# Reordering the start and the first pair's layer-norm work, and writing three quarters of the last product by rows of tokens

## The chip, the cores and the metric

The kernel runs on one core of a Trainium2 chip. The core has a matrix engine (PE, with its weight loads shown apart as PEld), a vector engine (DVE), an activation engine (ACT), a general engine (POOL) and a sequencer that issues transfers (SP); ACT and POOL issue transfers too. Each engine works through its own instructions in program order and waits on semaphores for the others. The metric is device time in microseconds (us); the median over several runs counts.

## The reference

For eight batches of T = 512 tokens with H = 256 features the reference computes, all in fp32:

```
nx       = layer_norm(x) * gamma + beta
weights  = softmax((nx Wq)(ctx Wk)^T / 16)          # 64 context rows a batch
evidence = weights (ctx Wv)
combined = [nx, evidence, anchor]                   # anchor: one row a batch, the same for all tokens
probs    = softmax(combined router_W + router_b)    # 3 experts
h_e      = silu(combined e_w1[e] + e_b1[e])         # 512 wide
routed   = sum_e probs_e (h_e e_w2[e] + e_b2[e])
g        = sigmoid(silu(combined gate_w1 + gate_b1) gate_w2 + gate_b2)
out      = x + g * (routed out_w + out_b)
```

## The kernel before

The eight batches are worked in four pairs (`j` = 0 to 3, batches 2j and 2j+1). Features lie on partitions and tokens along the free axis, so a product of one 128-feature block with 512 tokens fills one PSUM bank. For each pair the kernel runs `gate_layer`, then `expert_layer` for experts 0, 1 and 2, then `outputs`. The products of a pair's two batches are shared by Winograd's form of a 2 by 2 block product: seven products in place of eight, with sums and differences of the inputs (`combine_x`) and of the weights (`combine_weights`, `combine_second` on POOL). In an expert layer `nx_product(n, 1..7)` names the seven products of group `n`; U, Y and Z are the PSUM banks in which they collect. `keep_part` (ACT) copies a part out of a bank, `add` (DVE, L827) adds a later one, `silu` (ACT, L821) finishes a chunk, and `weigh` (DVE, L872 and L868) multiplies finished chunks by the router's probabilities from a list of debts `late`.

All instructions are traced by hand in one order (`manual_schedule`), so each engine's queue is the order of the Python calls. In the loop over pairs `put(within, (e, point), step, ...)` hangs a step on a point of expert layer `e`: points W, A, B, C, D come in that order, and steps of one point run in the order of the puts. Work for the next pair is placed so in this pair's layers. For pair 0 that is:

- `statistics` (DVE) for batches 2 and 3, `deviation` (ACT, two square roots, with a change of the activation table),
- `normalize(b)` (DVE, L549 and L552: a reciprocal and four instructions of 256 columns), which overwrites x; `store_x(b)` (SP, four transfers) writes the result to DRAM and `regroup_x(b)` (SP, eight transfers) reads it back in blocks of 32 by 32 for `transpose_blocks` (DVE, L612) in `outputs`,
- `router_part(b)` (DVE, L590: four sums along x).

Before the loop stands the start: the loads, layer norm and transposes of pair 0 by PE, its scores and softmax. `turn_weights(0)` (DVE, L689 and L691, five block transposes) turns the softmax weights so that PE can use them in `evidence`; `anchor_rows(g)` multiplies the anchors by a first-layer weight on PE (L433) and transposes the result out of its PSUM bank on DVE (L438); `combine_x(0, ..., (i,))` makes one of the four differences (L624), number 2 in place over the second batch's first block. `misc()` hands out spare PSUM banks in turn, so a product that takes a bank must wait until the bank's last reader is done.

The last pair's end in `outputs` is written out apart. `finish_early` prepares r11 and r21 (residual and gate folded in), `experts(...)` is one second-layer product of six steps, `half_experts(y, n)` makes half of the first batch's first block, 256 tokens in the free axis with features on partitions. `finish_tokens(r11, ...)` turns it round on PE, by products with the identity that add r and the gated product in PSUM, copies and stores rows of tokens. `finish_late(r21, u, ...)` gates, adds, transposes in blocks of 32 and stores (four transfers on the ACT and SP queues). All these results use tiles of the tag `yb`, which has two buffers. Each fp32 product shows as two records on PE.

Of the kernel before, what the change touches and what calls it, by code (L numbers as in the profile page):

```python
# [8 lines left out]
F32 = mybir.dt.float32  # L9
AF = mybir.ActivationFunctionType  # L10
ALU = mybir.AluOpType
# [5 lines left out]
def kernel(  # L17
# [51 lines left out]
    nc = tc.nc  # L69
    P = 128  # L70
    B, T, H = x.shape
# [3 lines left out]
    NT = T // P  # L75
# [15 lines left out]
    work = ctx.enter_context(tc.tile_pool(name="work", bufs=2))  # L91
# [6 lines left out]
    def bank(i, name):  # L98
        return psum.tile([P, 512], F32, tag=f"b{i}", name=name)
# [4 lines left out]
    def misc(name):  # L104
        spare.append(spare.pop(0))
        return bank(spare[-1], name)
# [6 lines left out]
    ident = const.tile([P, P], F32, tag="ident", name="ident")  # L113
# [76 lines left out]
    r = 0  # L190
# [340 lines left out]
    S = {}  # L531
# [152 lines left out]
    def turn_weights(j):  # L684


        wT, w = work.tile([P, T], F32, tag="wT", name=f"wT_{j}", bufs=1), S["w", j]
        S["wT", j] = wT
        nc.vector.transpose(wT, w.rearrange("p g j c -> p (g j c)"))  # L689
        for i, h in SIDES:  # L690
            nc.vector.transpose(  # L691
                wT[side(i, 1 - h), h * NH : (h + 1) * NH],
                w[side(i, h), 1 - h, :, :].rearrange("p j c -> p (j c)"),
            )
# [91 lines left out]
    def product(ps, lhsT, rhs, start=False):  # L786

        nc.tensor.matmul(ps, lhsT, rhs, start=start, stop=True, skip_group_check=not start)  # L788
# [43 lines left out]
    def hidden(j, q, k, i):  # L832
        return S["h", i, 2 * q // RC][:, (2 * q + k) % RC, :]
# [165 lines left out]
    def outputs(j, steps):  # L999
# [7 lines left out]
        hg = [[S["hg", i, k] for i in range(2)] for k in range(2)]  # L1007
# [14 lines left out]
        u, z, y = (bank(i, f"ps_g{n}_{j}") for n, i in (("u", 0), ("z", 2), ("y", 4)))  # L1022
# [19 lines left out]
        NQ = NE // 2  # L1042
        pb = S["pb", j]

        def a(q, i, k):
            return w2o[:, 2 * q + k, i * P : (i + 1) * P]
# [60 lines left out]
        def gated(ps, i, row, ts):  # L1107
            g = S["hg", row, i][:, ts]
            nc.vector.tensor_tensor(g, ps, g, ALU.mult)
            return g  # L1110
# [4 lines left out]
            nc.vector.transpose(g, r)  # L1115
            store(g, i, row, slice(0, T), (nc.scalar, nc.sync))

        def finish_tokens(r, ps, i, row, n):

            ts = slice(n * T // 2, (n + 1) * T // 2)  # L1120
            pt = [misc(f"pt_out_{n}_{t}")[:, :P] for t in range(NT // 2)]
            for t in range(NT // 2):
                lo = n * T // 2 + t * P
                nc.tensor.matmul(pt[t], r[:, lo : lo + P], ident, start=True, stop=False)
            g = gated(ps, i, row, ts)
            y = work.tile([P, NT // 2, P], F32, tag="yb", name=f"y_{n}")
            for t in range(NT // 2):
                lo = n * T // 2 + t * P
                nc.tensor.matmul(pt[t], g[:, t * P : (t + 1) * P], ident, start=False, stop=True)
                (nc.scalar.copy if t else nc.vector.tensor_copy)(y[:, t, :], pt[t])  # L1130
                (nc.scalar if t else nc.sync).dma_start(
                    out[2 * j + row, lo : lo + P, i * P : (i + 1) * P], y[:, t, :]
                )

        r11, r22, r12, r21 = (
            bias_sum(f"r{i + 1}{row + 1}", i, row) for i, row in ((0, 0), (1, 1), (0, 1), (1, 0))
# [29 lines left out]
            run("P4")  # L1166
            return

        def half_experts(ps, n):
            ts = slice(n * T // 2, (n + 1) * T // 2)  # L1170
            for q in range(NQ):
                product(ps[:, : T // 2], a(q, 0, 1), hidden(j, q, 1, 0)[:, ts], start=q == 0)

        subtract((0, 1), ((1, 0), (0, 1)))
        experts(z, combo(S4), 1, 1)
# [2 lines left out]
        finish(r12, z, 0, 1)  # L1178
        experts(u, lambda q: a(q, 1, 0), 0, 0)
        finish(r22, u, 1, 1)  # L1180
        half_experts(y, 0)
        experts(u, lambda q: a(q, 1, 1), 0, 1)
        finish_tokens(r11, y[:, : T // 2], 0, 0, 0)
        y = bank(2, "ps_y3")
        half_experts(y, 1)
        finish_late(r21, u, 1, 0)
        finish_tokens(r11, y[:, : T // 2], 0, 0, 1)


    with tc.manual_schedule(engines=None):  # L1190
# [44 lines left out]
        spread_router_rows(0)  # L1235
        softmax(0)
        value_weights(0, 0, nc.vector.tensor_copy)
        turn_weights(0)
        combine_x(0, nc.vector, (2,))
        anchor_rows(E)  # L1240
        anchor_rows(0)
        combine_x(0, nc.vector, (3,))
        combine_weights(1)
        combine_weights(2)
# [8 lines left out]
        for j in range(NP):  # L1253


            within, between = {}, {}

            def put(where, n, step, *args):
                where.setdefault(n, []).append(lambda: step(*args))

            if j == 0:
                put(within, "gate", value_weights, 0, 1)
                put(within, (0, "A"), anchor_rows, 1)
                put(within, (0, "A"), router_logits, 0)
                put(within, (0, "A"), load_second, 1)
                put(within, (0, "B"), second_bias)
                put(within, (0, "C"), transpose_second, 0)
                put(within, (0, "C"), anchor_columns, 1)
                put(within, (0, "C"), anchor_rows, 2)
                put(within, (0, "C"), router_exp, 0)  # L1270
                put(within, (0, "D"), router, 0)
                put(within, (0, "C"), load_second, 2)
                put(within, (0, "D"), second_layer, 0)
                put(within, (0, "D"), spread_probabilities, 0)
                put(within, (0, "D"), combine_second, 0)
                put(within, (1, "A"), transpose_second, 1)
                put(within, (1, "B"), second_layer, 1)
                put(within, (1, "B"), combine_second, 1)
                put(within, (1, "C"), transpose_second, 2)
                put(within, (1, "C"), anchor_columns, 2)  # L1280
                put(within, (1, "D"), second_layer, 2)
                put(within, (1, "D"), combine_second, 2)
            if j:
                put(within, "gate end", spread_probabilities, j)
            if j and j + 1 < NP:
                put(within, (0, "B"), statistics, 2 * j + 3, 0, NT)
            put(within, (0, "C" if j == 0 else "B"), value_weights, j, 2)
            put(within, (1, "C"), load_x_blocks, 2 * j)
            put(within, (2, "A"), gate_differences, j)
            put(within, (2, "C"), load_x_blocks, 2 * j + 1)  # L1290
            if j + 1 < NP:
                b0, b1 = 2 * j + 2, 2 * j + 3
                if j == 0:
                    put(within, "gate", load_x, b0)
                    put(within, "gate", load_x, b1)
                if j + 2 < NP:
                    put(between, "begin", load_x, b0 + 2)
                    put(between, "begin", load_x, b1 + 2)
                put(within, (0, "A" if j else "D"), statistics, b0, 0, NT)
                if j == 0:  # L1300
                    put(within, (1, "A"), statistics, b1, 0, NT)
                for i in range(2):
                    put(within, (0, "D") if j else (1, "C"), deviation, j + 1, i)
                for b, n in ((b0, (1, "W") if j else (1, "D")), (b1, (1, "W") if j else (2, "W"))):
                    put(within, n, normalize, b)
                    put(within, n, store_x, b)
                put(within, (1, "A") if j else (2, "A"), router_part, b0)
                put(within, (1, "C") if j else (2, "A"), regroup_x, b0)
                put(within, (1, "D") if j else (2, "C"), router_part, b1)
                put(between, "begin", transpose_blocks, b0)  # L1310
                put(between, "gate", regroup_x, b1)
                put(between, "begin", value_weights, j + 1, E)
                put(between, "begin", store_router_rows, j + 1)
                put(between, "begin", spread_router_rows, j + 1)
                put(between, "P5", transpose_blocks, b1)
                put(between, "P2", scores, j + 1)
                put(between, "P2", combine_x, j + 1, nc.gpsimd)
                put(between, "P7", softmax, j + 1)
                put(between, "P7", value_weights, j + 1, 0)
                put(between, "P7", router_logits, j + 1)  # L1320
                put(between, "P3", value_weights, j + 1, 1)
                put(between, "P3", turn_weights, j + 1)
                put(between, "P3", router_exp, j + 1)
                put(between, "P4", router, j + 1)
            gate_layer(j, within)
            for e in range(E):
                expert_layer(j, e, within)
            outputs(j, between)


# [32 lines left out]
```

## Time and profile before

| what | us |
|---|---|
| median of 3 runs | 472.14 (472.06 to 472.33) |
| the profiled execution, its own time | 472.42 |
| the span of that execution in the profile | 470.6 |
| PE busy in the span | 461.1 (98%) |
| DVE busy | 362.1 (77%) |
| ACT busy | 213.3 (45%) |
| POOL busy | 95.0 (20%) |
| last transfer issued, landed (from the span's start) | 467.29, 469.08 |

The profile is of one execution; 1.8 us of its time lie around the span. PE's clock was granted in full almost throughout (0.999). A busy time counts an instruction from start to end; PE's records overlap, so the spacing of their starts is the better measure of PE's pace. A line such as "92.00 0.68 DVE L827" in a timeline gives the start and the duration in us, the engine and the source line, then the operation, the tile written, the tiles read, the shapes, how many instructions are merged, and in brackets the idle time ahead of it with what ended it.

### The profile page before, as it was taken

What the parts mean: (1) busy time and instruction counts of PE and PEld (TensorE: products, weight loads), DVE (VectorE), ACT (ScalarE), POOL (GpSimd) and SP (SyncE); (2) the same over time, 40 slices, a digit from 0 to 9 for tenths busy, and PEclk for the clock granted to TensorE, in tenths of its full rate; (3) what the DMA queues carried; (4) which work ended last, traced back from release to release, by engine and by line L of the source; (5) the groups of instructions that cost most, each with busy time, mean ns of one, the idle gap of its engine ahead of it and who ended that gap; (6) DMA issues with size and microseconds to landing.
All of it is one profiled execution on the core that took longest, in us unless ns stands there. A gap on an engine that the chain in (4) does not pass through costs nothing.

```text
span 470.6 us, 4723 instructions
## 1 busy us (share of the span) xinstructions
PE 461.1 (98%) x1455; PEld 209.8 (45%) x1455; DVE 362.1 (77%) x669; ACT 213.3 (45%) x368; POOL 95.0 (20%) x133
## 2 busy tenths in 40 slices
PE   9989999989999999999999999999999999999996
PEld 7534546334444344444444344444444344444454
DVE  3875646999899659978889669888989724787972
ACT  3335655548221476458220476458130455457000
POOL 6536123201072300001062300001062300000020
PEclk9999999999999999999999999999999999999999
DMA  9998830375111424732011333712011480000013
GB/s 277 288 166 152 123 136 0 80 139 94 7 22 22 80 101 103 124 87 45 6 24 22 58 121 79 123 23 45 7 22 22 69 201 0 0 0 1 0 22 67
DMA packets 119351, 34.86 MB, mean 74 GB/s; under 512 B 106060, under 2 KB 116352, under 8 KB 118816
## 3 DMA queue, kind: packets, MB, share of 16 engines
q1 hardware_dynamic: 115312, 27.02, 29.5%
q0 software_dynamic: 2128, 6.78, 5.0%
q10 hardware_dynamic: 1888, 0.79, 0.6%
q8 instruction: 11, 0.18, 0.2%
q14 instruction: 12, 0.10, 0.1%
HBM read 27.17 MB, written 7.39 MB: 73 GB/s over the span
## 4 chain that ended last, share of the span: by engine, by line
PE 67%; DVE 26%; issue 3%; DMA 3%; POOL 0%; ACT 0%; DVEq 0%; POOLq 0%; ACTq 0%
PE ps_u L788 32%; PE ps_z L788 12%; PE ps_y L788 12%; DVE h L1063 5%; PE ps_gu L788 3%; DVE h L872 3%; PE ps_vw L763 3%; DVE r L1094 2%; DVE yb L1095 2%; DVE r L1093 2%; DVE wT L691 1%; PE ps_w2o L494 1%; PE ps_gz L788 1%; DMA scr_small<-in_L_xcond_router_W_dram 1%; DMA scr_small<-in_L_xcond_e_b_dram 1%
## 5 line engine op out<-in xcount | busy, mean ns | idle before, releaser
L872 DVE TENSOR_TENSOR h<-h,pb 128x512 f32<-128x512 f32 x96 | 61.9, 693 | 6.0 <-ACT h L821 6.0
L788 PE MATMUL ps_u<-h,w2o 128*128 128x512 f32 x144 | 64.1, 594 | 0.0
L788 PE MATMUL ps_u<-nxT,w 128*128 128x512 f32 x112 | 55.9, 608 | 0.5 <-ACT h L830 0.5
L821 ACT ACTIVATE h<-h,abias 128x512 f32<-128x512 f32 x72 | 49.2, 718 | 15.1 <-DVE h L827 14.7
L788 PE MATMUL ps_z<-wT,vw 64*128 64x512 f32 x104 | 49.5, 605 | 0.0
L1096 POOL TENSOR_TENSOR yb<-yb,xb 128x512 f32<-128x512 f32 x14 | 18.4, 1314 | 146.1 <-DVE yb L1095 120.6
L788 PE MATMUL ps_z<-h,w2s 128*128 128x512 f32 x96 | 42.6, 593 | 0.2 <-DVE r L1079 0.2
L830 ACT COPY h<-ps_u 128x512 f32<-128x512 f32 x48 | 27.9, 581 | 30.7 <-PE ps_u L788 30.4
L788 PEld LDWEIGHTS ps_u<-h,w2o 128*128 128x128 f32 x144 | 27.1, 190 | 32.6 <-issue 29.2
L827 DVE TENSOR_TENSOR h<-h,ps_y 128x512 f32<-128x512 f32 x24 | 16.4, 681 | 25.0 <-PE ps_y L788 25.0
L1063 DVE TENSOR_TENSOR h<-h,h 128x1024 f32<-128x1024 f32 x24 | 34.3, 1483 | 0.0
L408 POOL DMA_DIRECT2D vrd<-vw x8 | 5.0, 628 | 143.6 <-ACT vw L770 143.6
L788 PEld LDWEIGHTS ps_u<-nxT,w 128*128 128x128 f32 x112 | 19.8, 189 | 30.6 <-issue 24.4
L821 ACT ACTIVATE h<-ps_u,abias 128x512 f32<-128x512 f32 x24 | 16.5, 687 | 28.5 <-PE ps_z L788 28.2
L827 DVE TENSOR_TENSOR h<-h,ps_z 128x512 f32<-128x512 f32 x24 | 16.1, 683 | 16.8 <-PE ps_z L788 16.7
L788 PE MATMUL ps_u<-wT,vw 64*128 64x512 f32 x56 | 28.2, 617 | 0.5 <-DVE hg L827 0.4
L788 PEld LDWEIGHTS ps_z<-h,w2s 128*128 128x128 f32 x96 | 18.2, 190 | 23.5 <-issue 21.8
L788 PE MATMUL ps_z<-T,ws 128*128 128x512 f32 x56 | 28.6, 592 | 0.0
L788 PE MATMUL ps_y<-nxT,w 128*128 128x512 f32 x56 | 28.6, 592 | 0.0
L763 PE MATMUL ps_vw<-w,vT 128*128 128x512 f32 (+1 forms) x64 | 27.0, 544 | 1.5 <-DVE ar L438 1.5
L788 PE MATMUL ps_u<-T,w 128*128 128x512 f32 x56 | 26.7, 594 | 1.5 <-DVE h L827 1.5
L788 PE MATMUL ps_y<-wT,vw 64*128 64x512 f32 x56 | 27.0, 597 | 0.0
(233 smaller groups left out, 796.4 us busy)
## 6 DMA issues: line engine op xcount, KB each, us to landing
pb<-pd POOLq DMA_DIRECT2D x4, 1536.0 KB, 6.6
xb<-in_x_dram SPq DMA_DIRECT2D x64, 64.0 KB, 2.4
out_dram<-yb SPq DMA_DIRECT2D x56, 64.0 KB, 2.0
w<-in_L_xcond_e_w_dram SPq DMA_DIRECT2D x6, 512.0 KB, 9.3
x<-in_x_dram SPq DMA_DIRECT2D x24, 128.0 KB, 3.2
xd<-x SPq DMA_DIRECT2D x24, 128.0 KB, 2.3
xg<-xd SPq DMA_DIRECT2D x48, 64.0 KB, 2.3
scr_wa<-in_L_xcond_e_w_dram SPq DMA_DIRECT2D x3, 512.0 KB, 15.2
```

The source lines that it names most:

```text
L408: nc.gpsimd.dma_start(S["vrd", j][i].rearrange("e c -> c e"), S["vw", j][row_half(i), R0:])
L763: nc.tensor.matmul(ps, vT[:, k, j * 2 * CT : (j + 1) * 2 * CT], w1[:, KH + k, n0:n1], start=(k == 0), stop=(k == KH - 1),)
L788: nc.tensor.matmul(ps, lhsT, rhs, start=start, stop=True, skip_group_check=not start)
L821: nc.scalar.activation(h, h if src is None else src, AF.Silu, bias=abias[:, c, 2 * j + i : 2 * j + i + 1])
L827: nc.vector.tensor_tensor(h, h, part, ALU.add)
L830: nc.scalar.copy(chunk(n, i, d), part)
L872: nc.vector.tensor_tensor(h, h, S["pb", j][:, i, :, 2 * q // RC, :], ALU.mult)
L1063: nc.vector.tensor_tensor(d, p, m, ALU.subtract)
L1093: nc.vector.tensor_tensor(r, r, ps, ALU.add)
L1094: nc.vector.tensor_tensor(r, r, S["hg", row, i], ALU.mult)
L1095: nc.vector.transpose(yb, r)
L1096: nc.gpsimd.tensor_tensor(yb, yb, S["xb", 2 * j + row][:, i, :], ALU.add)
```

## The change

Three places change.

1. In the start, `anchor_rows(E)`, `anchor_rows(0)` and `combine_x(0, ..., (2,))` are called ahead of `turn_weights(0)`, not behind it.
2. For pair 0, `deviation` moves from point C to point B of expert layer 1. `normalize` and `store_x` of both batches are at point C of layer 1 (before: batch 2 at D of layer 1, batch 3 at W of layer 2). `regroup_x(2)` is at D of layer 1 (before: A of layer 2). `router_part(2)` is at C of layer 2 (before: A of layer 2), ahead of `router_part(3)`, which stays there. For the later pairs all points stay as they are.
3. In the last pair's end only the first 128 tokens of the split block keep the old way (`finish_tokens`, one tile). For the other 384 the gate and r11 are turned round ahead of time (`turn_rest`: six PE transposes into two banks, two ACT copies), and the product itself is made with tokens on partitions (`token_experts`: the hidden chunk is the weight operand and the 128 columns of `w2o` the moving one). `finish_rows` multiplies and adds on DVE, in two instructions of 128 by 128, and stores.

```diff
-        def finish_tokens(r, ps, i, row, n):
-
-            ts = slice(n * T // 2, (n + 1) * T // 2)
-            pt = [misc(f"pt_out_{n}_{t}")[:, :P] for t in range(NT // 2)]
-            for t in range(NT // 2):
-                lo = n * T // 2 + t * P
-                nc.tensor.matmul(pt[t], r[:, lo : lo + P], ident, start=True, stop=False)
-            g = gated(ps, i, row, ts)
-            y = work.tile([P, NT // 2, P], F32, tag="yb", name=f"y_{n}")
-            for t in range(NT // 2):
-                lo = n * T // 2 + t * P
-                nc.tensor.matmul(pt[t], g[:, t * P : (t + 1) * P], ident, start=False, stop=True)
-                (nc.scalar.copy if t else nc.vector.tensor_copy)(y[:, t, :], pt[t])
-                (nc.scalar if t else nc.sync).dma_start(
-                    out[2 * j + row, lo : lo + P, i * P : (i + 1) * P], y[:, t, :]
-                )
+        def finish_tokens(r, ps, i, row):
+
+            pt = misc("pt_out")[:, :P]
+            nc.tensor.matmul(pt, r[:, :P], ident, start=True, stop=False)
+            g = gated(ps, i, row, slice(0, P))
+            nc.tensor.matmul(pt, g, ident, start=False, stop=True)
+            y = work.tile([P, P], F32, tag="yb", name="y_tokens")
+            nc.scalar.copy(y, pt)
+            nc.scalar.dma_start(out[2 * j + row, :P, i * P : (i + 1) * P], y)
...
-        def half_experts(ps, n):
-            ts = slice(n * T // 2, (n + 1) * T // 2)
+        def turn_rest(r):
+
+            rest = work.tile([P, 2, NT - 1, P], F32, tag="xg", name="rest", bufs=1)
+            for n, part in enumerate((S["hg", 0, 0], r)):
+                pt = misc(f"pt_rest_{n}")[:, : T - P]
+                for t in range(1, NT):
+                    nc.tensor.transpose(pt[:, (t - 1) * P : t * P], part[:, t * P : (t + 1) * P], ident)
+                nc.scalar.copy(rest[:, n, :, :].rearrange("p t c -> p (t c)"), pt)
+            return rest
+
+        def token_experts(ps, t):
+
             for q in range(NQ):
-                product(ps[:, : T // 2], a(q, 0, 1), hidden(j, q, 1, 0)[:, ts], start=q == 0)
+                product(ps, hidden(j, q, 1, 0)[:, t * P : (t + 1) * P], a(q, 0, 1), start=q == 0)
+
+        def finish_rows(rest, ps, t, queue):
+            y = work.tile([P, P], F32, tag="yb", name=f"y_rows_{t}")
+            nc.vector.tensor_tensor(y, ps, rest[:, 0, t - 1, :], ALU.mult)
+            nc.vector.tensor_tensor(y, y, rest[:, 1, t - 1, :], ALU.add)
+            queue.dma_start(out[2 * j, t * P : (t + 1) * P, :P], y)
...
-        half_experts(y, 0)
+        for q in range(NQ):
+            product(y[:, :P], a(q, 0, 1), hidden(j, q, 1, 0)[:, :P], start=q == 0)
+        rest = turn_rest(r11)
         experts(u, lambda q: a(q, 1, 1), 0, 1)
-        finish_tokens(r11, y[:, : T // 2], 0, 0, 0)
-        y = bank(2, "ps_y3")
-        half_experts(y, 1)
+        finish_tokens(r11, y[:, :P], 0, 0)
+        tokens = [bank(b, f"ps_tokens_{b}")[:, :P] for b in (2, 0, 5)]
+        for t in range(1, NT):
+            token_experts(tokens[t - 1], t)
         finish_late(r21, u, 1, 0)
-        finish_tokens(r11, y[:, : T // 2], 0, 0, 1)
+        for t in range(1, NT):
+            finish_rows(rest, tokens[t - 1], t, nc.scalar if t % 2 else nc.sync)
...
-        turn_weights(0)
-        combine_x(0, nc.vector, (2,))
         anchor_rows(E)
         anchor_rows(0)
+        combine_x(0, nc.vector, (2,))
+        turn_weights(0)
         combine_x(0, nc.vector, (3,))
...
                 for i in range(2):
-                    put(within, (0, "D") if j else (1, "C"), deviation, j + 1, i)
-                for b, n in ((b0, (1, "W") if j else (1, "D")), (b1, (1, "W") if j else (2, "W"))):
-                    put(within, n, normalize, b)
-                    put(within, n, store_x, b)
-                put(within, (1, "A") if j else (2, "A"), router_part, b0)
-                put(within, (1, "C") if j else (2, "A"), regroup_x, b0)
+                    put(within, (0, "D") if j else (1, "B"), deviation, j + 1, i)
+                for b in (b0, b1):
+                    put(within, (1, "W") if j else (1, "C"), normalize, b)
+                    put(within, (1, "W") if j else (1, "C"), store_x, b)
+                put(within, (1, "C") if j else (1, "D"), regroup_x, b0)
+                put(within, (1, "A") if j else (2, "C"), router_part, b0)
                 put(within, (1, "D") if j else (2, "C"), router_part, b1)
```

## The prediction

> **What bounds the kernel now.** I read the page first, then PE's own waits, then the timelines of the three places that the diff touches. On the page two lines matter:
>
> ```profile
> PE 461.1 (98%) x1455; PEld 209.8 (45%) x1455; DVE 362.1 (77%) x669; ACT 213.3 (45%) x368; POOL 95.0 (20%) x133
> DMA  9998830375111424732011333712011480000013
> ```
>
> PE is the bound, so a change pays only where PE stands still or where the end comes after PE. Slices 6 and 7 of the DMA row (70 to 94 us) are nearly empty: transfers put there meet no traffic. PE's waits from 10 to 130 us:
>
> ```profile
> PE ps_u L788 <- DVE h L827: 1.5, 1, 1.5
> PE ps_vw L763 <- DVE ar L438: 1.5, 1, 1.5
> PE ps_u L788 <- ACT h L830: 0.5, 1, 0.5
> ```
>
> These three are at 98.34, 32.13 and 93.97 us. From 130 us to the end's 462 us, PE's starts leave no gap above 0.4 us. The first stop, PE and DVE:
>
> ```profile
> 29.59 1.02 PE L788 MATMUL ps_z<-nxT,ws 128*128 128x512 f32 x2
> 32.13 1.98 PE L763 MATMUL ps_vw<-w,vT 128*128 128x512 f32 x4 [1.52 <-DVE ar L438]
> 28.48 0.71 DVE L689 STREAM_TRANSPOSE wT<-w 128x512 f32<-128x512 f32 x1
> 29.23 1.78 DVE L691 STREAM_TRANSPOSE wT<-w 32x256 f32<-32x256 f32 x4
> 31.03 0.69 DVE L624 TENSOR_TENSOR nxT<-nxT 128x512 f32<-128x512 f32 x1
> 31.64 0.44 DVE L438 STREAM_TRANSPOSE ar<-ps_ar 128x64 f32<-128x64 f32 x2
> ```
>
> The value product needs a bank that L438 empties only after L689, L691 and L624. The second stop, and what DVE does up to the next meeting with PE:
>
> ```profile
> 92.60 0.69 DVE L996 TENSOR_TENSOR hg<-hg,hg 128x512 f32<-128x512 f32 x1
> ...
> 97.00 0.68 DVE L827 TENSOR_TENSOR h<-h,ps_y 128x512 f32<-128x512 f32 x1
> 97.60 1.28 DVE L827 TENSOR_TENSOR h<-h,ps_u 128x512 f32<-128x512 f32 x2
> ...
> 106.84 0.69 DVE L1016 TENSOR_TENSOR hg<-g_r,ps_gz 128x512 f32<-128x512 f32 x1 [0.68 <-PE ps_gz L788]
> 107.71 0.69 DVE L1016 TENSOR_TENSOR hg<-g_r,ps_gu 128x512 f32<-128x512 f32 x1 [0.18 <-PE ps_gu L788]
> ...
> 118.41 3.49 DVE L1063 TENSOR_TENSOR h<-h 128x1024 f32<-128x1024 f32 x3
> ```
>
> DVE is full from 74.0 to 127.7 us but for 0.86 us. PE's S2 product starts at 119.69, just behind the first L1063: there DVE, not PE, sets the pace. The end:
>
> ```profile
> 462.93 2.76 PE L788 MATMUL ps_y<-h,w2o 128*128 128x256 f32 x12
> 466.20 0.71 PE L1129 MATMUL pt_out<-ident,hg 128*128 128x128 f32 x4
> 467.29 0.36 ACTq L1131 DMA_DIRECT2D out_dram<-y  x1
> ```
>
> The last store is issued at 467.29 and lands 1.8 us later, at 469.08; what follows is fixed.
>
> **What the Trainium skill says.** "SBUF — State Buffer", Who interferes with whom: a DVE instruction with two SBUF inputs and a GpSimd one that reads SBUF exclude each other. The trace agrees: three L872 at 80.56 take 2.95 us beside POOL's `combine_second` (80.87 to 85.2), against 0.69 for one alone. "DMA: Bandwidth & Descriptors", Anatomy of one DMA: most of a fixed 2 us is the write's receipt, so a buffer is free only at landing. The small stores here land after 1.6 to 1.8 us. "TensorE: Matmul & The Clock Gate", Back-to-back issue gap: loads and products overlap, spacing depends on both. Here four records with 128 columns (462.04 to 462.48) come at 0.11 us each, load included. "ScalarE: Activation LUTs", What ACT_TABLE_LOAD costs: 1283 ns; the trace has 1.28.
>
> **Part 1, the start: -1.78 us.** PE's order stays. On DVE the two L438 come at 28.48 (0.44), the difference 2 to 29.6, `turn_weights` (0.71 + 1.78) to 32.1, difference 3 to 32.7. The value product starts in step at 30.45 (0.43 a record after 29.59 and 30.02), not at 32.13; a stop also costs 0.10 on restart (32.13 to the next load 32.67, not 0.43). Sum 1.78. Next in line: `evidence` needs the turned weights, due at 33.12 instead of 34.90, ready at 32.1; 1.0 us of cover. The value copy on ACT and all DVE adds follow PE. What is not moved, the loads, has slack: the router rows land by about 41 and are read at 43.98 (then 42.2), second-layer weights by 43 and read at 50.38. PE has no idle from there to 90 and DVE's full stretch starts when PE releases it at 74.0, so the gain lasts. Bounds: 1.4 (a load binds) to 1.8.
>
> **Part 2, pair 0's layer norm: -1.03 us.** Square roots: on ACT nothing lies between the old and new place, both follow the `w2o` copy at 73.14; table load, two roots, done 75.54; cost 0. `normalize` of both batches (0.2 + 4 x 0.35 = 1.55 each) now follows L486 and L443, 76.85 to 79.95, ahead of ten weighings. Behind them wait the weighings, then two `add` of Z (86.30 to about 87.75) and ACT's two `silu` behind those (to 89.8, needed by nobody before 91.4). `add` of Y at 92.00 has the same work ahead of it as before, so the 0.78 us stop at 93.97 stays. POOL still meets two-input instructions at 80.87: same 1.7 us of contention, taken as 0 (+-0.3). SP's eight stores leave at 78.5 and 80.0, not at 86.41 and 91.52, the eight reads follow by 87; the queue's next work is later anyway. POOL's memset (0.11) is covered by its idle time.
>
> The four sums of batch 2 (`router_part`, L590, 0.47 each with the read of the accumulator, 95.26 to 97.00) leave this place: Y's second add runs at 95.26, U's two at 95.86 and 96.46. PE's product 4, due at 96.65, waits for the first: released at 96.6 instead of 98.3. PE gains up to 1.79. But both batches' sums now come in one piece up to 100.54, and everything on DVE behind them is where it was, until the gate: L1016 no longer waits, 105.47, 106.07, 106.67, transposes at 107.28 for 108.31. That is 1.03 us, and L1063 and PE's S2 product move by just that (119.69 to 118.66); PE, 1.79 ahead, stands 0.76 there. After it DVE idles 2.6 us at 130.29, so 1.03 stays. Bounds: 0.5 (contention) to 1.79 (DVE finds slack).
>
> **Part 3, the end: +0.45 us.** PE before its last full product: 12 records at 0.11 (1.32) for 2.59, plus six transposes (eight took 0.87 at 19.25) 0.66: -0.61, so that product ends at 461.43, not 462.04. Two ACT copies of 384 columns (512 take 0.58) lie in ACT's idle time. Then four records 0.44 and 36 at 0.11: tokens ready on PE at 463.19, 464.51, 465.83. DVE: `finish_late` 461.63 to 463.78, its stores on ACT to 464.76; rows 1 at 463.75 to 464.36, store at 464.79.
>
> The price is in the buffers. `yb` has two. The tiles r12, r22, tokens, rows 1, rows 2, rows 3 take them in turn, so the multiplication of rows 3 overwrites rows 1 and must await its landing. No wait of this kind shows before; bounds: 464.79 + 1.7 = 466.5 if it overtakes, 467.4 if it queues fully behind the `finish_late` stores, whose landings take 2.4 to 2.6 us. I take 467.1, as it is behind two of them on its queue. Then multiply and add (0.29 each, nearest row the 128x128 copy, + 0.03) and issue: 467.8, landed 469.55. Against 469.08 that is +0.45; bounds -0.1 to +0.8. Without the wait: product seen at 466.03, issued 466.67, landed 468.4, -0.7.
>
> **Sum:** 472.42 - 1.78 - 1.03 + 0.45 = 470.06 for the profiled execution. The median of the runs is 0.28 lower: 469.8.
>
> **Rivals.** *A, more:* rows 3 doesn't wait (the buffers go otherwise), or pair 0 keeps all of 1.79. The first alone gives 472.14 - 1.78 - 1.03 - 0.7 = 468.6, the second alone 472.14 - 1.78 - 1.79 + 0.45 = 469.0, both 467.9. For: PE's gap is 1.79. Against: two buffers, and 119.69. *B, less:* contention or the late Z adds eat part 2, or the landing is late: -1.78 - 0.3 + 0.8, 470.9. *C, slower:* weight loads set the pace of the 48 records with 128 columns. The groups give 190 ns for one load, and 256 columns run at 0.215. At 0.215 the end is 48 x 0.105 = 5.0 later than the unwaited 468.4: 473.4, +4.3; with -2.81 the median is 473.6. It decides from about 0.18 us a record. Against: the identity products and transposes at 0.11. *D, no change:* a load that I take for early paces the start, so that part 1 returns nothing: -1.03 + 0.45 = -0.58, with B's losses -0.3 + 0.8 = +0.5, so 471.6 to 472.6. For: the DMA row is at 9 up to 24 us. Against: from 33 to 90 us no wait of PE or DVE ends on a transfer.
>
> **Numbers.** Forecast 0.56, A 0.18, B 0.16, C 0.04, D 0.06. 0.2% (0.94 us) is about what a measurement of this kernel can tell from no change. Faster by more: forecast, A, B: 0.90; within: D, 0.06; slower: C, 0.04. The predicted time is the forecast's, 469.8. The range takes in A's single cases and B with a little beyond: 468.3 to 471.0; it leaves out A's double case, C and D.
>
> **What would show it.** Right: no wait of L763 on L438, evidence near 33.1; no wait of PE on L827 near 96.6 but a longer one on L1063, near 117 in the new clock; a DVE wait on a store from `yb` ahead of the last multiplication of 128 by 128, about 1.1 us. Wrong: 128-column products at 0.2 us; the same gap at 98 with DVE full ahead of it; a last store that lands before 468.4 less 2.8.

## The result and the profile after

| | us |
|---|---|
| after, median of 14 runs | 471.11 (470.96 to 471.42) |
| before, median of 14 runs beside them | 472.37 (472.02 to 474.72) |
| ratio after to before | 0.9965, 95% interval 0.9953 to 0.9977 |
| the profiled execution of after: its time, its span | 471.00, 468.87 |

The kernel is faster, by less than forecast. The ratio is one of means, and three of the runs of before lay at 474.4 to 474.7: it says 1.65 us, the medians say 1.26. By the ratio, the 472.14 from which the prediction started becomes 470.5 (469.9 to 471.1), by the medians 470.9. Both lie inside its range of 468.3 to 471.0, near its upper end, and above its 469.8; the median of after itself, 471.11, lies 0.1 above the range.

Page of after, busy time and DMA row, then PE's waits from 10 to 130 us (total, times, longest):

```profile
PE 459.8 (98%) x1473; PEld 209.8 (45%) x1473; DVE 363.7 (78%) x672; ACT 214.0 (46%) x369; POOL 97.6 (21%) x133
...
DMA  8989933532012405812011414702011570000013
```

```profile
PE ps_u L788 <- ACT h L830: 0.8, 1, 0.8
PE ps_u L788 <- DVE h L1063: 0.8, 1, 0.8
```

PE is still the bound. Of its three stops two are gone, those on L438 and L827. The one on L830 has grown from 0.5 to 0.8, and L1063 is new at 116.97, the place that the prediction gave it. The timeline of after, at the start (PE, DVE):

```profile
29.29 1.02 PE L788 MATMUL ps_z<-nxT,ws 128*128 128x512 f32 x2
30.14 1.88 PE L763 MATMUL ps_vw<-w,vT 128*128 128x512 f32 x4
...
32.81 0.69 PE L788 MATMUL ps_y<-wT,vw 64*128 64x512 f32 x1
...
28.19 0.45 DVE L438 STREAM_TRANSPOSE ar<-ps_ar 128x64 f32<-128x64 f32 x2
...
30.02 1.80 DVE L691 STREAM_TRANSPOSE wT<-w 32x256 f32<-32x256 f32 x4
```

The value product follows at PE's pace (0.85 us after the line above it), since L438 comes first; the turned weights are ready at 31.8, ahead of `evidence` at 32.81. The layer-norm stretch (DVE, POOL):

```profile
80.86 1.10 DVE L868 TENSOR_TENSOR h<-h,h 128x512 f32<-128x512 f32 x1
81.89 3.48 DVE L872 TENSOR_TENSOR h<-h,pb 128x512 f32<-128x512 f32 x3
...
90.21 0.68 DVE L827 TENSOR_TENSOR h<-h,ps_y 128x512 f32<-128x512 f32 x1
...
104.40 0.68 DVE L1016 TENSOR_TENSOR hg<-g_r,ps_gz 128x512 f32<-128x512 f32 x1
...
105.60 1.29 DVE L612 STREAM_TRANSPOSE nxT<-xg 128x512 f32<-128x512 f32 x2
...
78.78 2.63 POOL L233 TENSOR_TENSOR w2s<-w2o 128x256 f32<-128x256 f32 x1 [4.17 <-ACT w2o L499]
```

DVE's two-input instructions stretch beside POOL's `combine_second`, and POOL's first instruction takes 2.63 us for 0.95 before. At the gate L1016 no longer waits. The end (PE, ACT's queue, DVE):

```profile
459.18 4.18 PE L788 MATMUL ps_tokens<-w2o,h 128*128 128x128 f32 x36
...
462.22 3.93 ACTq L1181 DMA_DIRECT2D out_dram<-y_rows  x2
...
461.57 0.29 DVE L1179 TENSOR_TENSOR y_rows<-ps_tokens,rest 128x128 f32<-128x128 f32 x1 [0.47 <-DMA out_dram<-y_tokens]
...
465.14 0.29 DVE L1179 TENSOR_TENSOR y_rows<-ps_tokens,rest 128x128 f32<-128x128 f32 x1 [2.35 <-DMA out_dram<-y_rows]
```

DVE stands idle for 2.35 us, up to 465.14, until rows 1 have landed; PE was done at 463.4, so 1.8 us of this lie behind PE's end. The last store is issued at 465.79 and lands at 467.36.

To compare executions I divide them at fixed places: the first `ps_vw` record behind L438 ("start"), the beginning of the last z product ("z": 443.89 before, 441.19 after; PE runs in step with small constant gaps from 130 us up to there), the landing of the last store, the end of the span, the time. From the last landing to the end of the span is the "tail".

| stretch | forecast | measured |
|---|---|---|
| up to `evidence` (34.90 to 32.81) | -1.78 | -2.09 |
| from there to z | -1.03 | -0.61 |
| from z to the last landing (25.19 to 26.17) | +0.45 | +0.98 |
| from there to the end of the span (1.57 to 1.51) | 0 | -0.06 |
| outside the span (1.77 to 2.13) | 0 | +0.36 |
| sum (472.42 to 471.00) | -2.36 | -1.42 |

### The profile page after: what moved, and what is told of

Read it like the earlier page. It is cut to its first block, busy times and chain, and to the rows that moved or that the text cites. A ratio compares the mean times of both kernels' runs of the same rounds, so it can differ in the third digit from the quotient of the medians.

```text
span 468.9 us, 4767 instructions
## 1 busy us (share of the span) xinstructions
PE 459.8 (98%) x1473; PEld 209.8 (45%) x1473; DVE 363.7 (78%) x672; ACT 214.0 (46%) x369; POOL 97.6 (21%) x133
## 4 chain that ended last, share of the span: by engine, by line
PE 70%; DVE 25%; issue 3%; DMA 1%; ACT 0%; DVEq 0%
PE ps_u L788 31%; PE ps_z L788 12%; PE ps_y L788 11%; DVE h L1063 5%; DVE h L872 4%; PE ps_vw L763 3%; PE ps_gu L788 3%; DVE r L1094 2%; DVE yb L1095 2%; DVE r L1093 2%; PE ps_w2o L494 1%; PE ps_gz L788 1%; DVE wT L691 1%; DVE h L868 1%; DVE r L1073 1%
## 5 line engine op out<-in xcount | busy, mean ns | idle before, releaser
L830 ACT COPY h<-ps_u 128x512 f32<-128x512 f32 x48 | 27.9, 581 | 30.5 <-PE ps_u L788 30.1
L827 DVE TENSOR_TENSOR h<-h,ps_y 128x512 f32<-128x512 f32 x24 | 16.4, 683 | 25.0 <-PE ps_y L788 21.1
L1063 DVE TENSOR_TENSOR h<-h,h 128x1024 f32<-128x1024 f32 x24 | 34.3, 1483 | 0.0
L827 DVE TENSOR_TENSOR h<-h,ps_z 128x512 f32<-128x512 f32 x24 | 16.1, 684 | 16.8 <-PE ps_z L788 16.7
L788 PE MATMUL ps_u<-T,ws 128*128 128x512 f32 x56 | 26.7, 594 | 0.0
```

Of the source, the lines that this page charges most:

```text
L827: nc.vector.tensor_tensor(h, h, part, ALU.add)
L830: nc.scalar.copy(chunk(n, i, d), part)
L1063: nc.vector.tensor_tensor(d, p, m, ALU.subtract)
```

## The experiments

**Each part by itself.** Each kernel is the one before with a single part of the change: `start_only` part 1, `norm_only` part 2, `end_only` part 3.

```diff
# start_only
-        turn_weights(0)
-        combine_x(0, nc.vector, (2,))
         anchor_rows(E)
         anchor_rows(0)
+        combine_x(0, nc.vector, (2,))
+        turn_weights(0)
# norm_only: only the edits of deviation, normalize, store_x, regroup_x, router_part
# end_only: only finish_tokens, turn_rest, token_experts, finish_rows and their calls
```

> The kernel before with part 1 alone. Theory (each part does its own sum): 1.8 us faster than before, the value product no longer waits for L438, every later meeting of PE and DVE moves by the same 1.8. Rival (a load or the DVE stretch of pair 0 takes it back): under 1.0 us faster, with a new wait of PE between 33 and 120 us.

> The kernel before with part 2 alone. Theory: 0.6 us faster than before, PE's stop at 98.34 gone, the stop at 93.97 some 0.3 longer, a new stop of about 1.0 behind L1063. Rival as forecast: 1.0 us faster, contention with POOL unchanged. Second rival (DVE has slack): 1.8 us faster, no new stop.

> The kernel before with part 3 alone. Theory: 1.0 us slower than before, DVE waiting 2.3 us for a store ahead of the last multiplication of 128 by 128. Rival (the end's cost in the changed kernel came from what ran before it): within 0.4 us of before.

| kernel | median (before: 472.51) | ratio, 95% interval | start to z | z to last landing | outside span |
|---|---|---|---|---|---|
| before | | | 411.76 | 25.19 | 1.77 |
| `start_only` | 470.61 | 0.9954, 0.9939 to 0.9969 | 411.66 | 25.18 | 1.73 to 1.82 |
| `norm_only` | 471.92 | 0.9986, 0.9976 to 0.9996 | 411.14 | 25.19 | 1.72 to 1.84 |
| `end_only` | 473.69 | 1.0021, 1.0014 to 1.0028 | 411.77 | 26.24 | 2.09 to 2.21 |

PE's waits from 10 to 130 us in `start_only`:

```profile
PE ps_u L788 <- DVE h L827: 1.5, 1, 1.5
PE ps_u L788 <- ACT h L830: 0.5, 1, 0.5
```

The same of `norm_only`:

```profile
PE ps_vw L763 <- DVE ar L438: 1.8, 1, 1.8
PE ps_u L788 <- ACT h L830: 0.8, 1, 0.8
PE ps_u L788 <- DVE h L1063: 0.8, 1, 0.8
...
```

DVE in the timeline of `end_only`, ahead of rows 3:

```profile
468.08 0.29 DVE L1179 TENSOR_TENSOR y_rows<-ps_tokens,rest 128x128 f32<-128x128 f32 x1 [2.43 <-DMA out_dram<-y_rows]
```

Each part takes away just its own stop and makes just its own wait, and the product of the three ratios is 0.9961, the whole change's 0.9965. Part 1 gains, part 2 gains a little, part 3 loses about 1.0. (The old order in the start loses 0.10 more behind its stop, so "start to z" is 411.66 in `start_only` and 411.76 before.)

**The wait for buffers.** `own_rows` is the kernel after, with a buffer of its own for each of the three row tiles.

```diff
-            y = work.tile([P, P], F32, tag="yb", name=f"y_rows_{t}")
+            y = work.tile([P, P], F32, tag=f"yr{t}", name=f"y_rows_{t}", bufs=1)
```

> The changed kernel with a buffer of its own for each of the three row tiles. Theory (the landing of rows 1 holds the end): 1.7 us faster than the changed kernel, last multiplication about 0.2 us behind PE's last record. Rival (the last store is held by the queue, behind the stores of finish_late): under 0.5 us faster, the last store landing over 2.3 us after its issue.

Median 469.14 (468.93 to 469.41), ratio 0.9922 (0.9906 to 0.9938): 1.97 us under the median of after. DVE in its timeline:

```profile
463.36 0.29 DVE L1179 TENSOR_TENSOR y_rows<-ps_tokens,rest 128x128 f32<-128x128 f32 x1 [0.72 <-PE ps_tokens L788]
```

DVE now waits for PE alone; the last store lands 24.45 us after z, not 26.17. So part 3's new product is worth 0.74 against 25.19 before, and the reuse of two buffers, which cost 1.72, turned that into a loss of 0.98. In the profiled executions another 0.36 us come back outside the span (in all runs it is 1.73 to 1.85 here, 2.09 to 2.17 after).

**The sums along x.** `sums_back` is the kernel after with the four sums of batch 2 (`router_part`) in their old place, all else as changed.

```diff
-                put(within, (1, "A") if j else (2, "C"), router_part, b0)
+                put(within, (1, "A") if j else (2, "A"), router_part, b0)
```

> The changed kernel with router_part of batch 2 back at point A of layer 2. Theory (DVE's idle time at the gate is all that the move can give back): PE stops 1.7 us again near 96 us, DVE idles 0.9 us at L1016 again, the stop behind L1063 falls to 0.25 or less, and the sum is only 0.9 us slower than the changed kernel. Rival (PE's stop counts in full): 1.7 us slower.

Median 472.24 (472.03 to 473.1), ratio 0.9992 (0.9985 to 0.9999). Start to z takes 411.98, for 411.05 after: 0.93. PE's longest wait from 10 to 130 us, and DVE in its timeline:

```profile
PE ps_u L788 <- DVE h L827: 1.5, 1, 1.5
```

```profile
105.33 0.69 DVE L1016 TENSOR_TENSOR hg<-g_r,ps_gz 128x512 f32<-128x512 f32 x1 [0.68 <-PE ps_gz L788]
106.20 0.69 DVE L1016 TENSOR_TENSOR hg<-g_r,ps_gu 128x512 f32<-128x512 f32 x1 [0.18 <-PE ps_gu L788]
```

PE again waits 1.5 us for L827 ahead of product 4, and DVE again waits at the gate: 0.68 + 0.18 of the 0.93. So the move of the sums is worth what DVE no longer waits and not PE's gap, as the prediction argued. The rest of part 2, the earlier layer norm, costs 0.3 by itself (411.98 against 411.66 in `start_only`, which has the same start).

**Who runs beside POOL.** `norm_beside_pool` changes the order after once more: five weighings go ahead of the two `normalize`, so that these run beside `combine_second`, and the others behind it.

```diff
+                if j == 0:
+                    put(within, (1, "C"), weigh, j, 5)      # ahead of normalize
...
-            weigh(j, 6 if j or e > 1 else 10)
+            weigh(j, 6 if j or e > 1 else 5)
```

> The changed kernel with five of the ten weighings ahead of the two normalizations and five behind, so that L552, with one SBUF tensor input, stands beside POOL's combine. Theory (only instructions with two SBUF inputs and POOL exclude each other): DVE's loss beside POOL falls from 2.0 us to about 0.6, 1.3 us faster than the changed kernel. Rival (L552 excludes POOL as well, as its 0.24 us beside POOL in the kernel before may say): the loss stays at 1.5 to 2 us, under 0.5 us faster.

Median 470.53 (470.48 to 471.72), ratio 0.9954 (0.9937 to 0.9972); start to z 410.48, 0.57 less than after, under half of what I expected and nearer to the rival. DVE in its timeline:

```profile
77.96 1.79 DVE L552 TENSOR_SCALAR x<-x,mv,rstd 128x256 f32<-128x256 f32 x4
79.87 2.51 DVE L552 TENSOR_SCALAR x<-x,mv,rstd 128x256 f32<-128x256 f32 x4
```

Four of these take 1.38 us undisturbed. Though they read one tensor from SBUF, they lose 1.54 us beside POOL, where the weighings in their place lost 2.0 (below). "SBUF — State Buffer", Who interferes with whom, in the Trainium skill has `tensor_scalar` among the operations that can take the shared ports in a two-port mode, when their operands allow it. That they lose time beside POOL is what this trace shows; whether they ran in that mode no run shows. I had counted on one input being safe.

**POOL's work at another place.** `late_combine` is the kernel after with `combine_second(2)` moved into layer 2, behind a POOL copy of one column that waits for a weighing there.

```diff
+    def wait_for_weighed(q):
+        mark = work.tile([P, 1], F32, tag="mark", name="mark", bufs=1)
+        nc.gpsimd.tensor_copy(mark, hidden(0, q, 0, 0)[:, :1])
...
-                put(within, (1, "D"), combine_second, 2)
+                put(within, (2, "D"), wait_for_weighed, 4)
+                put(within, (2, "D"), combine_second, 2)
```

> The changed kernel with POOL's combine_second(2) held back by a one-column POOL copy of a chunk that DVE weighs at 102 us, so that it runs beside DVE instructions with one SBUF input. Theory (POOL's contention sets how far DVE falls behind): the ten weighings take 2.0 us less, PE's stops at 92.17 and 116.97 go, 1.9 us faster than the changed kernel. Rival (the stop behind L1063 comes from DVE's own amount of work): the stop at 92.17 goes but L1063 stays where it is, under 0.5 us faster. Second rival: the S1 product waits for the late combine near 114 us, slower.

Median 467.75 (467.7 to 468.0), ratio 0.9893 (0.9876 to 0.9911). DVE and POOL in its timeline (lines are four further down in the file):

```profile
80.74 0.69 DVE L872 TENSOR_TENSOR h<-h,h 128x512 f32<-128x512 f32 x1
81.35 1.89 DVE L876 TENSOR_TENSOR h<-h,pb 128x512 f32<-128x512 f32 x3
...
100.85 0.73 POOL L233 TENSOR_TENSOR w2s<-w2o 128x256 f32<-128x256 f32 x1
```

From the first L868 to the next `add` DVE needs 3.14 us, for 5.15 after (80.86 to 86.01): the contention cost 2.0 us. Start to z falls from 411.05 to 409.03, the same 2.0, and both of PE's stops on L830 and L1063 shrink to 0.15 us or nothing. At 100.85 POOL runs beside DVE instructions that read PSUM, and both keep their times. But the span fell by 3.31, and this explains 2.02 (the start was 0.12 earlier): 0.81 came between z and the last landing, and 0.36 in the tail. Nothing in the edit's purpose explains those.

**Both.** `both` is `late_combine` with the edit of `own_rows`.

> The changed kernel with own buffers for the three row tiles and with POOL's combine held back. Theory: the two gains lie in different places and add, 1.8 + 1.9 = 3.7 us faster than the changed kernel. Rival: DVE's gain is absorbed, 1.8 us faster in all.

Median 466.78 (466.38 to 466.87), ratio 0.9869 (0.985 to 0.9889): of the kernels here the fastest, 4.3 us under the median of after, where 3.7 was expected. Start to z 409.05, z to the last landing 24.45. The two single gains, 1.97 and 3.36, don't add in full: with own buffers the end is as in `own_rows`, so the 0.81 of `late_combine` has no place left.

**Why the stores landed sooner.** The mark tile in `late_combine` moves all tiles behind it by 32 bytes of each partition, the `hg` tiles too. From these, and not from `yb`, `finish_late` stores pieces of 128 bytes. In the program of the kernel after they start at byte 210912 of a partition, 224 past a multiple of 256; with the mark they start at a multiple of 256. `pad32` and `pad64` are the kernel after with an unused tile of 32 or 64 bytes ahead of `hg`; it moves `hg` and one tile of hidden chunks, which lies behind `hg` and is never stored:

```diff
+        if j == 0:
+            pad = hpool.tile([P, 8], F32, tag="pad", name="pad")     # pad64: [P, 16]
+            nc.gpsimd.memset(pad, 0.0)                               # pad32_8, pad64_8: eight times
         for i in range(2):
             for k in range(KH):
                 S["hg", i, k] = hpool.tile(...)
```

> The changed kernel with one unused tile of 32 bytes a partition ahead of the four `hg` tiles, so that these alone start 32 bytes further on: a multiple of 64 bytes, where they were 32 past one. Order of work unchanged but for one memset of POOL (about 0.1 us). What is open: with `late_combine` the store of rows 1 landed about 2.1 us after its issue, in the changed kernel 2.8, and the three quarters of a microsecond were gained beside what the step in POOL explains. Theory: it is the place in SBUF that `finish_late`'s 128-byte stores read from (the small mark tile had moved everything behind it by 32 bytes); then the issue of the last store comes 0.7 to 0.9 us sooner relative to PE's last full product, DVE waits about 1.5 us ahead of rows 3 in place of 2.35, and the median is 470.2 to 470.4. Rival: the order of work on POOL or the queues did it; then the landing stays at 2.8 us and the median at 471.1.

> The same with a tile of 64 bytes: the `hg` tiles are moved, but stay 32 bytes past a multiple of 64. Theory (multiple of 64 bytes): landing of rows 1 again 2.8 us after issue, DVE's wait 2.35 us, median 471.1 as the changed kernel. Rival (any move of the tiles, or the added memset, does it): as with 32 bytes, 470.2 to 470.4.

Medians 470.47 (470.3 to 470.54) and 470.3 (470.01 to 470.56), ratios 0.9958 (0.9946 to 0.9971) and 0.9953 (0.9939 to 0.9966). The two are as good as equal, as the rival had it, but because another thing moved. DVE in the timeline of `pad32`:

```profile
462.71 0.29 DVE L1182 TENSOR_TENSOR y_rows<-ps_tokens,rest 128x128 f32<-128x128 f32 x1 [1.47 <-DMA out_dram<-y_tokens]
```

The DMA view of `pad32` from 459 to 463 us (queue: packets, MB, share; then a store with its KB and its us to landing):

```profile
q14 instruction: 1, 0.01, 1.1%
...
out_dram<-y_tokens ACTq DMA_DIRECT2D x1, 64.0 KB, 2.6
```

The one packet of 8 KB on queue 14 is a fetch of instructions. It came at 460.94 (460.99 in `pad64`). Of the 128 pieces of the tokens' store 120 went out from 460.73 to 461.05 and the other 8 only from 461.62 on; that store landed in 2.58 us instead of 1.58, and rows 1, which share its buffer, waited for it. By then `finish_late`'s stores were almost through, and the rest went quicker: z to the last landing is 25.89 and 25.91, for 26.17 after. The place of `hg` still shows in the packets of `finish_late` on ACT's queue: with no rows beside them they go out within 1.40 us in `pad32` and 1.76 in `pad64`. In the kernel after, the fetch comes at 468.85, behind all the stores. With eight memsets in POOL's idle time it comes at 452.4 to 452.5, ahead of them:

> `pad32` with its one memset issued eight times (all in POOL's idle stretch from 45.4 to 52 us, 0.8 us). With one memset POOL's last 8 KB packet of instructions was fetched at 460.94, on a DMA engine that carried part of the store of the first 128 tokens: that store landed 2.58 us after its issue in place of 1.58, and rows 1 had to wait for it. In the changed kernel this packet comes at the very end (468.85). Eight memsets should bring it ahead of 459. Theory (place of `hg` in SBUF matters, and the packet of instructions separately): the store of the tokens lands in 1.6 us, rows 1 in about 2.1, DVE's wait ahead of rows 3 is about 1.5 us, 0.7 to 0.9 us are gained there, and 0.36 us in the tail between last landing and end of the span (1.15 for 1.51, as in every run so far where that packet comes early): median 469.8 to 470.1. Rival (only the packet of instructions counts): rows 1 land in 2.8 us, median 470.7.

> `pad64` with eight memsets: the packet of instructions as in `pad32_8`, the `hg` tiles 32 bytes past a multiple of 64 as in the changed kernel. Theory: only the tail is shorter, rows 1 land in 2.8 us, DVE waits 2.35 us, median 470.7 to 470.8. Rival (the place of `hg` doesn't matter): equal to `pad32_8` within 0.2 us.

DVE in the timeline of `pad32_8`, ahead of rows 3:

```profile
464.68 0.29 DVE L1183 TENSOR_TENSOR y_rows<-ps_tokens,rest 128x128 f32<-128x128 f32 x1 [1.53 <-DMA out_dram<-y_rows]
```

The same of `pad64_8`:

```profile
465.45 0.29 DVE L1183 TENSOR_TENSOR y_rows<-ps_tokens,rest 128x128 f32<-128x128 f32 x1 [2.42 <-DMA out_dram<-y_rows]
```

| kernel | median | ratio, 95% interval | z to last landing | tail |
|---|---|---|---|---|
| after | 471.11 | 0.9965, 0.9953 to 0.9977 | 26.17 | 1.51 |
| `pad64_8` (32 past a multiple of 256) | 471.22 | 0.9971, 0.9959 to 0.9982 | 26.24 | 1.15 |
| `pad32_8` (a multiple of 256) | 470.35 | 0.996, 0.9946 to 0.9974 | 25.35 | 1.15 |

Between the last two only the size of the unused tile differs, and so the place of `hg`: 0.89 us at the last landing. The medians differ by 0.87, but the runs overlap (469.88 to 471.4 and 470.68 to 471.35), so it is the traces that decide. They agree across kernels: where the rows share `yb` and no fetch falls among the stores, z to the last landing is 25.35 and 25.36 in the two kernels with `hg` at a multiple of 256 (`pad32_8`, `late_combine`) and 26.17 to 26.24 in the five others. With own buffers the place no longer counts: 24.45 in `own_rows` (224 past) and in `both` (a multiple). The packets of `finish_late` on ACT's queue go out in 1.40 us (462.49 to 463.89) in `pad32_8` and in 2.29 (462.43 to 464.72) in `pad64_8`. "DMA: Bandwidth & Descriptors", How a descriptor splits into AXI transactions, in the Trainium skill says that a transaction starts at a multiple of 256 bytes. By this, at 224 or 32 past one, every second piece of 128 bytes would span two. The runs agree with that, but places other than 0, 32 and 224 weren't tried, so a step of 64 or 128 bytes would fit them as well.

In both kernels the tail is also 0.36 shorter with the early fetch, as it is by 0.3 or more in all six kernels in which the fetch comes ahead of the last landing (1.15 to 1.21, against 1.50 and more in the others). How the two hang together no run shows: the late fetch itself starts only at the end of the span. Both things happened in `late_combine`, with `hg` at a multiple of 256 and the fetch at 453.3, and they make up its 0.81 and 0.36. The medians of `pad32_8` and `pad64_8` lie 0.25 and 0.42 above what was expected; in their profiles the start comes 0.36 and 0.25 later than in that of after, which the edits don't touch.

## Why the prediction was right or wrong

**What bounds it.** Right. The two stops of PE that the change removes were the gain, and where part 2's gain ends (the gate, then L1063) was named.

**Part 1.** Right, in the profiled execution to the hundredth. `evidence` is 2.09 earlier, but 0.31 of it was there before the edit's place (PE's `ps_ar` at 25.22 before and 24.91 after; in the other kernels here it varies from 24.79 to 25.47); the rest is 1.78. `start_only` has the same.

**Part 2.** The path was right, two terms were mis-sized. Contention with POOL was "taken as 0 (+-0.3)": `add` of Y moved by -1.79 (92.00 to 90.21) where the start had given -2.09, so 0.30 was lost; with the layer norm ahead, the weighings and all of `combine_second` met. And the eight sums in one piece take a little longer than in two: L868 behind them moved by -1.67 (100.54 to 98.87), another 0.12 lost. 1.03 - 0.30 - 0.12 is the measured 0.61. The 1.7 us of contention that the prediction held fixed were the larger matter: with the 0.30 they are the 2.0 that `late_combine` returns.

**Part 3.** The wait was foreseen, its price was not: +0.45 stood where +0.98 was measured, and the sum had 1.15 us for the wait (from -0.7 to +0.45), which `own_rows` puts at 1.72. The product's end came as worked out (z to the end of the u product 17.55 for 18.15, so -0.60), 128 columns came at 0.11 us a record, and the unwaited end of -0.7 is `own_rows`' -0.74. The mis-sized term is the landing of rows 1: it came 2.83 us after the issue in the trace, where the sum had 2.3. The issue was 0.13 late too, since the tiles don't take the two buffers in plain turn, as written: the tokens' tile, rows 1 and rows 3 share one, and rows 2 have the other, so rows 1 waited for the tokens' landing. I took `finish_late`'s landings from before, where little followed them on the queues; here rows 1 stood behind their slow packets. The place of `hg` alone makes 0.89 us at the last landing (`pad32_8` against `pad64_8`), more than the whole 0.53 by which the sum was off.

**The sum.** It took what lies around the span as fixed; that grew by 0.36, which is the second term that was wrong. In every one of the nine kernels in which the row tiles share `yb` it is 2.09 to 2.21, and in the five without that 1.72 to 1.85, the kernel before among them. So it goes with the row tiles' shared buffers; what it is, no run shows, and it stays open.

**The rivals.** B's reasons, contention and a late landing, both came true, and its 470.9 is nearer to the measured time than the forecast. A's first case is `own_rows`. C is out: the 36 records take 4.18 us. D is out: part 1 returned all that it was given.

## What to carry to other kernels

Before a last store reuses a buffer, price the landing of the store that holds it, with everything queued ahead, and compare that with the SBUF for buffers of its own: here three tiles of 512 bytes a partition were worth 2 us. They also made the end independent of where `hg` lay. When DVE sets the pace, count POOL's instructions beside it as a cost that can be moved: four of them took 2.0 us from DVE, and 20 us later they disturbed nobody. An edit that adds a tile or an instruction also moves addresses and instruction fetches, so a gain beyond the step's own working should be tested with a kernel that moves only those.

## What the runs showed of the hardware that was not expected

- Two stores of 64 KB in 128-byte pieces from SBUF took 1.40 us of queue time from a multiple of 256 bytes (in all four kernels with this place). From 32 bytes past one they took 2.29 us with the stores of rows close behind them and 1.76 without.
- In the two kernels in which an 8 KB instruction fetch fell among the pieces of a 64 KB store, that store landed 1.0 us later (2.58 for 1.58). A fetch behind the last store goes with a tail that is 0.3 to 0.4 us longer.
- A run of two-input DVE instructions kept a POOL instruction of 0.73 us at work for 2.63, and lost 2.0 us itself beside four of them; one-input `TENSOR_SCALAR` lost 1.54 in the same place, while POOL's four kept to 0.73 to 0.80 there.
